# Small operations moved, and the token buffers kept as two pairs, in a two-layer attention kernel

## The chip, the cores and the metric

The kernel runs on one core of one Trainium2 chip. The metric is the device time of one execution in microseconds (us). A program of this kind is timed several times and the median is given; one more execution is recorded by the hardware profiler, and all durations of single instructions below come from that one.

## The reference

The input x has 32 x 128 tokens of 256 channels, all float32. Two layers follow each other.

```python
# layer 0: all 4096 tokens attend to each other, 8 heads of 32 channels
q = layernorm(h) * ln_g + ln_b
q = q @ wq.T + bq + sym_emb[:, None]            # one bias row for each n of 32
Q, K, V = q @ wQ.T + bQ, h @ wK.T + bK, h @ wV.T + bV
scores = Q K^T / sqrt(32);  scores[t_key > t_query] = -inf
h = h + alpha * ((softmax(scores) @ V) @ out_w.T + out_b)

# layer 1: attention in a band of 24 tokens, then a mixture of 8 experts
t = h.reshape(4096, 256)
z = layernorm(t)
logits = relu((z @ K) @ z.T + bias) - 10000 * (1 - band)
t = t + softmax(logits * temperature) @ z
x = layernorm(t);  w = softmax(x @ Wr + br)     # a share of each expert
y_e = relu(bn2(relu(bn1(x @ W1_e + b1_e)) @ W2_e + b2_e)) @ Wo_e + bo_e
t = t + sum_e w_e * y_e
```

## The kernel before

The function fast_kernel does the work; a general one stands by for inputs with large values. The order of instructions is written out by hand: each engine executes its own instructions in the order in which the program issues them, and SyncE (SP) issues nearly all DMAs, in one queue.

**Layer 0.** The 4096 queries, in the order of t, are cut into 8 blocks (b) of 512. A block has two units (b, g), g being one of two groups of four heads, and a unit has steps (b, g, k), k running over the tiles of 128 keys that the mask leaves. For n running over all steps, the loop

- computes scores of step n on TensorE: head 0 into the bank sa, heads 1 to 3 into three banks sb (`scores`, L1330; sb has two buffers);
- adds the products of the weights of step n - 2 with the values into av (`product`, L1420);
- takes the exponentials on ScalarE, in two instructions with `between` in the middle (`exps`, L1343 and L1345), into one of five buffers pt, and clears masked places on GpSimd (L1357). In each unit one step holds two part tiles that both need such clearing, and others hold one;
- adds the weights of step n - 1 on VectorE to an accumulator acc, in two halves of two heads each (`add`, L1371 to L1406). The first addition of a second unit has four parts (L1383, L1387), as it also takes over a tile from the unit before;
- issues one or more pieces of other work, from the generator `todo`, so many per block (`count`), in equal distances.

After a unit has ended, `close_sums` adds the accumulator's rows on TensorE (L1450), and sends them through SP (r16, L1481); five steps later `invert` takes the reciprocals on VectorE (L1489) and sends them through DRAM to all rows (flat, rec), and six steps later `scale` multiplies the result (L1502).

The work in `todo` is first `prep(b + 1)`, in four pieces: the next block is transposed (L984), and its keys, values and queries are projected (L993, L1039, L1012). In block 2 `output_weights` follows: it loads wo_n, alpha and outb, transposes wo_n, scales it by alpha into woT, and then multiplies bvb, the value bias spread over 128 columns, with woT (L1225) to correct outb (L1228). In block 3 `expert_norms` follows: it first calls `window`, which loads two scalars of layer 1 (temp, abias), builds the band bandb on GpSimd (L1237 to L1248) and clears the edges of big_t, then loads the batch norms' vectors, and transposes them in a second piece.

The first two blocks' deviations are computed ahead of layer 0; those of the other 24 tiles in block 1: after the last statistics, `root_rstd` adds 1e-5 on VectorE (L1542) and takes the root on ScalarE (L1545), with an exchange of the activation table before it and after it (L911). `send_rstd` spreads a block's deviations through DRAM (rstd, rb: L972, L976).

**Token buffers.** The pool tok has four buffers under one tag, xg. They hold, in the order of the loads: blocks 0 and 1 for the projections, blocks 2 to 7 for the statistics (named xs), blocks 2 and 3 again, block 4, then wo_n, then blocks 5, 6 and 7, and at last the tokens of layer 1's first four blocks, in which the results are built (tokens0 to tokens3; `load_tokens`, L896). Each load waits until the buffer's last contents were read. `tokens_at` names the steps at which tokens0 to tokens3 are loaded: three in block 5, one in block 6. `with_bias(n)` adds outb to tile n of them on GpSimd (L904): six in block 5, six in block 6, in the second unit, where

```python
if NBLK - 3 <= b < NBLK - 1 and g and 4 <= k < 4 + FIRST // 2:
    with_bias((b - NBLK + 3) * FIRST // 2 + k - 4)
```

**Layer 1.** A stretch written out by hand leads from layer 0 into it. Then 64 pairs of block and expert follow each other (`work`, `Layer`, `combine`), all on TensorE. `combine` multiplies half a block with Wo into one bank (L2137) and adds it to the tokens on VectorE, weighted by the expert's share (L2145); after the last expert it writes each tile out (L2150). Between these products a planner, `insert`, puts the jobs of the later blocks: projection, normalising (ScalarE, L1797), turning (transposes, L1813), keys, band scores, and the jobs that bound the values of the inputs (squares, columns: L2164, L2171). A job is issued once `later` us of the planner's own clock have passed since all that it needs (3.2, and 4.7 from the second block on).

Of the kernel before, what the change touches and what calls it, by code (L numbers as in the profile page):

```python
# [10 lines left out]
F32 = mybir.dt.float32  # L11
# [812 lines left out]
def fast_kernel(ctx: ExitStack, tc: tile.TileContext, ins: dict, out: bass.AP, narrow):  # L824
# [63 lines left out]
    big_t = big.tile([P, 2, NT + 2 * SIDE], F32, name="big_t")  # L888


    tok = ctx.enter_context(tc.tile_pool(name="tok", bufs=4))
# [34 lines left out]
    with ExitStack() as l0:  # L926
# [9 lines left out]
        def load_x(b, name, amid=()):  # L936
            xg = tok.tile([P, TPB, D], F32, tag="xg", name=f"{name}{b}")
            for tl in range(TT):
                if tl < len(amid):
                    amid[tl]()  # L940
                src = x[0][:, b * TPB * TT : (b + 1) * TPB * TT, :].rearrange(
                    "n (i tl) d -> tl n i d", tl=TT
                )[tl]
                nc.sync.dma_start(out=xg[tl * N : (tl + 1) * N], in_=src)
            return xg
# [255 lines left out]
        def output_weights(banks):  # L1201

            wo_n = tok.tile([P, TPB, D], F32, tag="xg", name="wo_n")[:, :2, :]
# [4 lines left out]
            nc.sync.dma_start(out=outb, in_=row(ins["L0_conv_out_b"]).to_broadcast([P, D]))  # L1208
            yield
# [10 lines left out]
            bvb = px.tile([P, 2, P], F32, tag="bvb", name="bvb", bufs=1)  # L1220
            for c in range(2):
                nc.vector.tensor_copy(bvb[:, c, :], colT[:, c, 6:7].to_broadcast([P, P]))
# [10 lines left out]
        def window():  # L1233

            nc.sync.dma_start(out=temp, in_=row(ins["L1_attn_temperature"]).to_broadcast([P, 1]))
            nc.sync.dma_start(out=abias, in_=row(ins["L1_attn_bias"]).to_broadcast([P, 1]))
# [12 lines left out]
            for z in (0, SIDE + NT):  # L1249
                nc.gpsimd.memset(big_t[:, :, z : z + SIDE], 0.0)  # L1250

        def expert_norms(banks):

            window()
# [11 lines left out]
            nc.vector.tensor_copy(bnT.rearrange("p c k -> p (c k)"), ps[:, : 2 * NB])  # L1266
            yield


        with ExitStack() as at:  # L1270
# [91 lines left out]
            def add(b, g, k):  # L1362
# [15 lines left out]
                if k == 1:  # L1378
                    first, lo = held[b, g, 0], parts[0][2]
                    if more:  # L1380
                        z = more[1][2]
                        for hs in HEADS:
# [3 lines left out]
                            )  # L1386
                            nc.vector.tensor_tensor(  # L1387
# [152 lines left out]
            def root_rstd():  # L1540
                cols = slice(2 * TPB, NTILE)
                nc.vector.tensor_scalar(  # L1542
                    rstd0[:, cols], mean0[:, cols, 1], 1e-5, None, op0=ALU.add
                )
# [30 lines left out]
            u, z = NBLK - 3, NBLK - 2  # L1575
            tokens_at = [(u, 0, 2), (u, 0, 4), (u, 1, 0), (z, 1, 0)]
            todo, done, count = iter(()), 0, 0
            later = {}
            for n in range(len(steps) + LAG + 1 + 16):
                if n < len(steps):  # L1580
                    b, g, k = steps[n]
                    own = sum(len(units[b, i]) for i in range(NGRP))
                    if g == 0 and k == 0:
# [9 lines left out]
                        if b == 2:  # L1593
                            todo, count = itertools.chain(todo, output_weights(banks)), 8
                        if b == 3:
                            todo, count = itertools.chain(todo, expert_norms(banks)), 7
# [26 lines left out]
                if n < len(steps):  # L1623
# [12 lines left out]
                    if (b, g, k) in tokens_at:  # L1636
                        nb = tokens_at.index((b, g, k))
                        load_tokens(
                            nb, tok.tile([P, TPB, D], F32, tag="xg", name=f"tokens{nb}")
# [5 lines left out]
                    for sb_, si in stat_at.get(n, ()):  # L1645
                        stats(sb_, si, xstat[sb_])
                        if (sb_, si) == (NBLK - 1, TPB - 1):
                            due = 1
                    if 1 < b < NBLK - 1 and not g and k == 1:
                        send_rstd(b + 1)  # L1650
                    if NBLK - 3 <= b < NBLK - 1 and g and 4 <= k < 4 + FIRST // 2:
                        with_bias((b - NBLK + 3) * FIRST // 2 + k - 4)
# [476 lines left out]
    def combine(ht, k, r2):  # L2129
# [3 lines left out]
        ps = bank(f"psy{k}_{r2}").rearrange("p (k d) -> p k d", k=2)  # L2133
        for i in range(2):
            r = 2 * r2 + i
            for c in range(2):
                nc.tensor.matmul(  # L2137
                    ps[:, i, :], lhsT=ht[:, c, r * P : (r + 1) * P],
# [3 lines left out]
        for i in range(2):  # L2142
# [3 lines left out]
                out=tokens(n), in0=ps[:, i, :], scalar=w[:, r, e : e + 1],  # L2146
# [235 lines left out]
    jobs, done_at = [], {}  # L2382
# [90 lines left out]
    jobs = [j for j in jobs if j[0] not in done_at]  # L2473

# [30 lines left out]
    def insert(passed):  # L2505
# [4 lines left out]
        while k < len(jobs) and few < 3:  # L2510
# [4 lines left out]
            if all(done_at.get(q, now) + later <= now for q in needs if q in known):  # L2515
# [111 lines left out]
```

## Time and profile before

| | us |
|---|---|
| median of 3 runs | 1494.84 (1494.55 to 1494.99) |
| the profiled execution, device time | 1492.53 |
| its span from the first to the last instruction | 1490.7 |
| TensorE (PE) busy in the span | 1457.9 |
| VectorE (DVE) busy | 1201.1 |
| ScalarE (ACT) busy | 936.5 |
| GpSimd (POOL) busy | 159.5 |
| mean granted clock of TensorE | 0.994 of full speed |

In the profile a row of the timeline has the start, the length, the engine, the line, the operation, what it writes and reads, the shape and the count; in brackets stands how long the engine was idle before it, and who ended that. PEld is TensorE's loading of weights, beside its products. SPq and ACTq are the engines' sequencers, which issue DMAs. In this execution block 2 of layer 0 runs from about 96 to 165 us, block 3 to about 246, block 5 from about 339 to 449, block 6 from there to about 577, and layer 1 begins near 710.

### The profile page before, as it was taken

To read this page: it belongs to the slowest core of one execution; us is meant where nothing else is said; L and a number is where in the kernel's file an instruction comes from. 1 tells how busy PE (TensorE), PEld (TensorE's weight loads), DVE (VectorE), ACT (ScalarE), POOL (GpSimd) and SP (SyncE) were. 2 spreads that over 40 slices of the span, in tenths; PEclk is the share of its full clock that TensorE was granted. 3 is DMA by queue.
4 is the path that set the end of the run, shared out by engine and by line. 5 is a ranking of instruction groups with operands and counts; after the bars stand their busy time and mean duration, and the time that the engine had idled before them with its cause. 6 is when DMAs were issued, how large, how long until landed. Compare 5 with 4: busy or idle time off the path is not lost.

```text
span 1490.7 us, 23636 instructions
## 1 busy us (share of the span) xinstructions
PE 1457.9 (98%) x8873; PEld 842.3 (56%) x8873; DVE 1201.1 (81%) x2189; ACT 936.5 (63%) x1357; POOL 159.5 (11%) x318
## 2 busy tenths in 40 slices
PE   9999999999999999999899999999999999999998
PEld 5333232232322232222557888888888888888887
DVE  4777788989999999999746787777777777777775
ACT  4776777879889879989454444445445544544443
POOL 2110112100200200000063012020011000000000
PEclk9999999999999999999999999999999999999999
DMA  6220101021000000000332333333433334334442
GB/s 136 51 45 19 30 10 30 9 41 39 1 15 23 1 9 1 8 9 1 119 119 94 121 121 110 120 115 122 134 112 124 106 121 138 112 121 125 130 148 66
DMA packets 96378, 110.15 MB, mean 74 GB/s; under 512 B 17950, under 2 KB 85233, under 8 KB 96257
## 3 DMA queue, kind: packets, MB, share of 16 engines
q1 hardware_dynamic: 93280, 106.87, 24.2%
q8 instruction: 72, 1.18, 0.4%
q0 software_dynamic: 1888, 0.91, 0.2%
q10 hardware_dynamic: 1088, 0.79, 0.2%
q14 instruction: 50, 0.40, 0.1%
HBM read 98.87 MB, written 8.53 MB: 72 GB/s over the span
## 4 chain that ended last, share of the span: by engine, by line
PE 83%; DVE 9%; ACT 4%; issue 2%; DMA 1%; POOL 1%; SPq 0%; ACTq 0%; DVEq 0%; POOLq 0%
PE psh L2076 22%; PE sa L1330 15%; PE av L1420 15%; PE psy L2137 13%; DVE acc L1406 2%; PE psv L1039 2%; PE psq L1012 2%; PE psk L1825 2%; PE psk L993 2%; PE sums L1450 1%; ACT h L2059 1%; PE sb L1330 1%; PE psh L2081 1%; PE pso L1515 1%; PE pss L1837 1%
## 5 line engine op out<-in xcount | busy, mean ns | idle before, releaser
L1406 DVE TENSOR_TENSOR acc<-acc,pt 128x1024 f32<-128x1024 f32 (+2 forms) x470 | 518.1, 1168 | 31.5 <-POOL pt L1357 16.2
L1345 ACT ACTIVATE pt<-sb 128x1536 f32<-128x1536 f32 (+1 forms) x265 | 382.6, 1444 | 1.7 <-PE sb L1330 1.7
L1330 PE MATMUL sa<-q,kT 32*128 32x512 f32 (+3 forms) x576 | 298.8, 605 | 4.5 <-ACT pt L1343 3.6
L1330 PE MATMUL sb<-q,kT 32*128 32x512 f32 (+3 forms) x1728 | 302.0, 604 | 0.0
L2059 ACT ACTIVATE h<-h,bshift,bscale 128x256 f32<-128x256 f32 x244 | 159.2, 699 | 219.1 <-DVE h L2118 219.0
L1420 PE MATMUL av<-pt,v 128*32 128x512 f32 (+3 forms) x2304 | 284.0, 573 | 3.3 <-POOL pt L1357 2.6
L2137 PE MATMUL psy<-wo,h 128*128 128x256 f32 x1024 | 243.6, 381 | 0.0
L2137 PEld LDWEIGHTS psy<-wo,h 128*128 128x128 f32 x1024 | 191.6, 190 | 31.9 <-issue 5.9
L1330 PEld LDWEIGHTS sa<-q,kT 32*128 32x128 f32 x576 | 86.7, 184 | 211.9 <-ACT pt L1343 176.7
L1343 ACT ACTIVATE pt<-sa 128x512 f32<-128x512 f32 (+1 forms) x265 | 158.2, 597 | 73.2 <-PE sb L1330 44.4
L1420 PEld LDWEIGHTS av<-pt,v 128*32 128x32 f32 x2304 | 48.0, 108 | 202.9 <-issue 178.0
L2145 DVE SCALAR_TENSOR_TENSOR tokens<-psy,w,tokens 128x256 f32<-128x256 f32 x256 | 111.0, 475 | 29.1 <-PE psy L2137 28.7
L2103 DVE TENSOR_TENSOR u<-psh,u 128x256 f32<-128x256 f32 x122 | 51.2, 420 | 100.6 <-ACT u L2102 100.3
L1357 POOL MEMSET pt<- 32x256 f32 (+4 forms) x123 | 52.3, 425 | 603.3 <-ACT pt L1345 526.4
L2059 ACT ACTIVATE h<-psh,bshift,bscale 128x256 f32<-128x256 f32 (+1 forms) x132 | 75.8, 576 | 49.7 <-PE psh L2076 43.3
L1330 PEld LDWEIGHTS sb<-q,kT 32*128 32x128 f32 x1728 | 91.0, 184 | 5.1 <-ACT pt L1345 3.8
L2076 PE MATMUL psh<-tx,s 128*128 128x256 f32 x366 | 89.1, 379 | 0.3 <-DVE tx L2049 0.3
L2102 ACT COPY u<-psh 128x256 f32<-128x256 f32 x122 | 43.9, 361 | 72.0 <-PE psh L2076 71.7
L2076 PE MATMUL psh<-th,s 128*128 128x256 f32 x366 | 89.0, 379 | 0.0
L2118 DVE TENSOR_TENSOR h<-psh,u 128x512 f32<-128x512 f32 x122 | 83.1, 681 | 3.2 <-PE psh L2076 3.0
L2076 PEld LDWEIGHTS psh<-tx,s 128*128 128x128 f32 x366 | 69.4, 190 | 10.2 <-DVE tx L2049 0.7
L2076 PEld LDWEIGHTS psh<-th,s 128*128 128x128 f32 x366 | 69.5, 190 | 9.5
(343 smaller groups left out, 1779.1 us busy)
## 6 DMA issues: line engine op xcount, KB each, us to landing
w<-in_L_ffn_W_dram SPq DMA_DIRECT2D x128, 256.0 KB
s<-kept SPq DMA_DIRECT2D x56, 512.0 KB
wo<-in_L_ffn_Wo_dram SPq DMA_DIRECT2D x64, 256.0 KB
xg<-in_x_dram SPq DMA_DIRECT2D x32, 128.0 KB
tokens<-in_x_dram SPq DMA_DIRECT2D x8, 512.0 KB
kept<-s SPq DMA_DIRECT2D x8, 512.0 KB
out_dram<-tokens SPq DMA_DIRECT2D x32, 128.0 KB
rec<-flat SPq DMA_DIRECT2D x60, 64.0 KB
```

Source lines behind the costliest of these rows:

```text
L1330: nc.tensor.matmul((sb[:, h - 1, :] if h else sa)[:, at : at + w], lhsT=kT[rows, gg, j * P : (j + 1) * P], rhs=q[rows, gg, lo : lo + w], s ...
L1343: nc.scalar.activation(pt[:, 0, used], sa[:, used], AF.Exp, scale=SCALE)
L1345: nc.scalar.activation(pt[:, 1:, used], sb[:, :, used], AF.Exp, scale=SCALE)
L1357: nc.gpsimd.memset(rows, 0.0)
L1406: nc.vector.tensor_tensor(acc[:, hs, cols], acc[:, hs, cols], pt[:, hs, at : at + w], op=ALU.add,)
L1420: nc.tensor.matmul(av[h * HD : (h + 1) * HD, lo : lo + w], lhsT=v[:, j, (g * HG + h) * HD : (g * HG + h + 1) * HD], rhs=pt[:, h, at : at + w],
L2059: nc.scalar.activation(dst, src, AF.Relu, bias=bshift[:, m, k : k + 1], scale=bscale[:, m, k : k + 1])
L2076: nc.tensor.matmul(ps, lhsT=w, rhs=x, start=start, stop=True, skip_group_check=True)
L2103: nc.vector.tensor_tensor(u, a[:, 1], u, op=ALU.add)
L2118: nc.vector.tensor_tensor(flat.rearrange("p (k c) -> p k c", k=2), self.q, self.u.unsqueeze(1).to_broadcast([P, 2, HB]), op=ALU.add,)
L2137: nc.tensor.matmul(ps[:, i, :], lhsT=ht[:, c, r * P : (r + 1) * P], rhs=wo[k][:, c, :], start=(c == 0), stop=(c == 1),)
L2145: nc.vector.scalar_tensor_tensor(out=tokens(n), in0=ps[:, i, :], scalar=w[:, r, e : e + 1], in1=tokens(n), op0=ALU.mult, op1=ALU.add,)
```

## The change

- The pool tok has two tags of two buffers each. The loads go to xa or xb: the statistics' blocks 2, 3, 6 and 7, block 4, wo_n, tokens0 and tokens1 to xb, all others to xa.
- tokens0 and tokens1 are loaded in block 3, and with_bias takes their eight tiles in block 3's second unit (k from 3 to 10). The four tiles of tokens2 follow in block 5's second unit (k from 6 to 9), and none in block 6.
- The first piece of output_weights (its loads, and now the copies to bvb) runs at the start of block 2, and the first piece of expert_norms (its loads, now with temp and abias) at the start of block 3, ahead of that block's own load. window is called after the batch norms' transposes. The edges of big_t are cleared at the program's start.
- The addition of 1e-5 for the 24 tiles is issued directly after their last statistics.
- The four parts of a second unit's first addition stand in another order.
- The last of the 64 pairs uses a bank for each tile in combine.
- The planner waits 4.7 us behind a normalised tile, and 6.0 behind a square.

```diff
+    for z in (0, SIDE + NT):
+        nc.gpsimd.memset(big_t[:, :, z : z + SIDE], 0.0)
-    tok = ctx.enter_context(tc.tile_pool(name="tok", bufs=4))
+    tok = ctx.enter_context(tc.tile_pool(name="tok", bufs=2))
...
         def load_x(b, name, amid=()):
-            xg = tok.tile([P, TPB, D], F32, tag="xg", name=f"{name}{b}")
+            late = b in ((2, 3, 6, 7) if name == "xs" else (4,))
+            xg = tok.tile([P, TPB, D], F32, tag="xb" if late else "xa", name=f"{name}{b}")
...
         def output_weights(banks):
-            wo_n = tok.tile([P, TPB, D], F32, tag="xg", name="wo_n")[:, :2, :]
+            wo_n = tok.tile([P, TPB, D], F32, tag="xb", name="wo_n")[:, :2, :]
...
             nc.sync.dma_start(out=outb, in_=row(ins["L0_conv_out_b"]).to_broadcast([P, D]))
+            bvb = px.tile([P, 2, P], F32, tag="bvb", name="bvb", bufs=1)
+            for c in range(2):
+                nc.vector.tensor_copy(bvb[:, c, :], colT[:, c, 6:7].to_broadcast([P, P]))
             yield
...
             yield
-            bvb = px.tile([P, 2, P], F32, tag="bvb", name="bvb", bufs=1)
-            for c in range(2):
-                nc.vector.tensor_copy(bvb[:, c, :], colT[:, c, 6:7].to_broadcast([P, P]))
             ps = banks("ps_ob", 1)[0][:, :D]
...
         def window():
-            nc.sync.dma_start(out=temp, in_=row(ins["L1_attn_temperature"]).to_broadcast([P, 1]))
-            nc.sync.dma_start(out=abias, in_=row(ins["L1_attn_bias"]).to_broadcast([P, 1]))
...
-            for z in (0, SIDE + NT):
-                nc.gpsimd.memset(big_t[:, :, z : z + SIDE], 0.0)
         def expert_norms(banks):
-            window()
+            nc.sync.dma_start(out=temp, in_=row(ins["L1_attn_temperature"]).to_broadcast([P, 1]))
+            nc.sync.dma_start(out=abias, in_=row(ins["L1_attn_bias"]).to_broadcast([P, 1]))
...
             nc.vector.tensor_copy(bnT.rearrange("p c k -> p (c k)"), ps[:, : 2 * NB])
+            window()
             yield
...
                                 live[b, g][:, hs, :z], first[:, hs, :z], pt[:, hs, :z],
                                 op=ALU.add,
                             )
+                        for hs in HEADS:
                             nc.vector.tensor_tensor(
                                 live[b, g][:, hs, z:], live[b, g][:, hs, z:], pt[:, hs, z:],
...
             def root_rstd():
                 cols = slice(2 * TPB, NTILE)
-                nc.vector.tensor_scalar(
-                    rstd0[:, cols], mean0[:, cols, 1], 1e-5, None, op0=ALU.add
-                )
...
-            u, z = NBLK - 3, NBLK - 2
-            tokens_at = [(u, 0, 2), (u, 0, 4), (u, 1, 0), (z, 1, 0)]
+            tokens_at = [(3, 0, 2), (3, 0, 9), (NBLK - 3, 1, 0), (NBLK - 2, 1, 0)]
...
                         if b == 2:
-                            todo, count = itertools.chain(todo, output_weights(banks)), 8
+                            more = output_weights(banks)
+                            next(more)
+                            todo, count = itertools.chain(todo, more), 7
                         if b == 3:
-                            todo, count = itertools.chain(todo, expert_norms(banks)), 7
+                            more = expert_norms(banks)
+                            next(more)
+                            todo, count = itertools.chain(todo, more), 6
...
                         nb = tokens_at.index((b, g, k))
+                        tag = "xb" if nb < 2 else "xa"
                         load_tokens(
-                            nb, tok.tile([P, TPB, D], F32, tag="xg", name=f"tokens{nb}")
+                            nb, tok.tile([P, TPB, D], F32, tag=tag, name=f"tokens{nb}")
                         )
...
                         if (sb_, si) == (NBLK - 1, TPB - 1):
+                            cols = slice(2 * TPB, NTILE)
+                            nc.vector.tensor_scalar(
+                                rstd0[:, cols], mean0[:, cols, 1], 1e-5, None, op0=ALU.add
+                            )
                             due = 1
...
-                    if NBLK - 3 <= b < NBLK - 1 and g and 4 <= k < 4 + FIRST // 2:
-                        with_bias((b - NBLK + 3) * FIRST // 2 + k - 4)
+                    if b == NBLK - 5 and g and 3 <= k < 3 + 2 * TPB:
+                        with_bias(k - 3)
+                    if b == NBLK - 3 and g and 6 <= k < 6 + FIRST - 2 * TPB:
+                        with_bias(2 * TPB + k - 6)
...
-        ps = bank(f"psy{k}_{r2}").rearrange("p (k d) -> p k d", k=2)
+        if k < len(work) - 1:
+            ps = bank(f"psy{k}_{r2}").rearrange("p (k d) -> p k d", k=2)
+            pss = [ps[:, i, :] for i in range(2)]
+        else:
+            pss = [bank(f"psy{k}_{r2}_{i}")[:, :D] for i in range(2)]
...
+    for name in bound_of:
+        slow["square", name] = 6.0
+    for n in range(NTILE):
+        slow["normalise", n] = 4.7
...
-            if all(done_at.get(q, now) + later <= now for q in needs if q in known):
+            if all(done_at.get(q, now) + max(later, slow.get(q, 0)) <= now for q in needs if q in known):
```

More of the change, by code (lines that the diff above doesn't have):

```diff
@@ L2137, in combine @@
                 nc.tensor.matmul(
-                    ps[:, i, :], lhsT=ht[:, c, r * P : (r + 1) * P],
+                    pss[i], lhsT=ht[:, c, r * P : (r + 1) * P],
                     rhs=wo[k][:, c, :],
@@ L2145, in combine @@
             nc.vector.scalar_tensor_tensor(
-                out=tokens(n), in0=ps[:, i, :], scalar=w[:, r, e : e + 1],
+                out=tokens(n), in0=pss[i], scalar=w[:, r, e : e + 1],
                 in1=tokens(n), op0=ALU.mult, op1=ALU.add,
@@ L2377, in fast_kernel @@
         with_bias(n)
-    jobs, done_at = [], {}
+    jobs, done_at, slow = [], {}, {}
     def job(name, cost, f, *needs):
```

## The prediction

> **What bounds the kernel now.** I read the page's first two parts, then the waits, then the timeline around each wait of TensorE, and last the table of stretches with the granted clock. The page says that TensorE is the bound everywhere:
>
> ```profile
> PE 1457.9 (98%) x8873; PEld 842.3 (56%) x8873; DVE 1201.1 (81%) x2189; ACT 936.5 (63%) x1357; POOL 159.5 (11%) x318
> PEclk9999999999999999999999999999999999999999
> ```
>
> So a moved small operation can only pay where TensorE stands idle (1490.7 - 1457.9 = 32.8 us, 6.9 of it after the last product), or where it is busy at a low clock, which the tenths hide. The timeline shows the idle places by the bracket behind a TensorE row. The five large ones of layer 0:
>
> ```profile
> 72.61 0.69 PE L1330 MATMUL sa<-q,kT 32*128 32x512 f32 x1 [2.04 <-ACT pt L1343]
> ...
> 145.57 0.63 PE L1213 MATMUL ps_wo<-ident,wo_n 128*128 128x128 f32 x4 [1.97 <-DMA wo_n<-in_L_conv_out_w_dram]
> ...
> 157.00 2.04 PE L1225 MATMUL ps_ob<-woT,bvb 128*128 128x256 f32 x4 [3.01 <-DVE bvb L1222]
> ...
> 232.25 1.51 PE L1420 MATMUL av<-pt,v 128*32 128x384 f32 x8 [2.61 <-POOL pt L1357]
> ...
> 521.31 0.69 PE L1330 MATMUL sa<-q,kT 32*128 32x512 f32 x1 [0.84 <-ACT pt L1343]
> ```
>
> What stands behind the first, the fourth and the fifth is one engine further back: ScalarE waits for an addition that VectorE has behind its sums, GpSimd is held by the band, and ScalarE waits for a buffer that VectorE has not yet read.
>
> ```profile
> 69.18 0.22 ACT L1545 ACTIVATE rstd<-rstd 128x24 f32<-128x24 f32 x1 [2.06 <-DVE rstd L1542]
> ...
> 222.66 7.25 POOL L1246 TENSOR_SCALAR bandb<-bandb,abias 128x160 f32<-128x160 f32 x1 [12.82 <-DMA abias<-in_L_attn_bias_dram]
> ...
> 520.66 0.60 ACT L1343 ACTIVATE pt<-sa 128x512 f32<-128x512 f32 x1 [1.60 <-DVE acc L1383]
> ```
>
> The stretches just after three of these waits carry a second loss. Their columns are length, busy time by engine, then the granted clock (0.50 here, 1.00 around them):
>
> ```profile
> 146.47:149.88 3.41, 3.41 (x28) 1.10 (x20) 2.76 (x3) 2.30 (x4) 0.00 (x0) 0.50 0.00 0
> 156.71:160.12 3.41, 3.12 (x12) 1.69 (x12) 1.31 (x6) 0.00 (x0) 0.00 (x0) 0.50 0.00 0
> 231.80:238.63 6.83, 6.38 (x38) 1.76 (x40) 6.26 (x8) 1.94 (x2) 0.40 (x1) 0.50 0.46 116
> ```
>
> TensorE is busy in them, and does half the work: they cost another 1.71, 1.56 and 3.19 us (half of the busy time).
>
> [...] idle times of 1.94 to 2.98 us were enough, while the 2.04 us at 70.6 drew nothing. [...] the band's addition (L1246) took 7.25 us beside a run of VectorE sums, and VectorE's 0.68 us halves (L1387) took 1.21 us beside the bias additions of L904 at 513 to 520. [...] the trace has 1.28 for both loads around the root (L1545, L911). The change keeps their number.
>
> **The change part by part**, each against the profiled execution.
>
> 1. *The addition of 1e-5 before the root* (L1542) goes directly behind the last statistics, which ended at 64.14. ScalarE's first table load ends at 65.84 + 1.28 = 67.12, so its 2.06 us wait goes; the second load and the key copies come as much earlier, and TensorE's 2.04 us with them. Next late is nothing above 0.1: the products before end at 70.57, and the exponential would then end at about 70.5. Gain 2.0 (1.2 to 2.1).
>
> 2. *wo_n loaded at block 2's start* instead of inside it: 1.94 + 1.71 = 3.65. Its three issues (0.58, 0.47, 0.43) now stand on SP ahead of the load of xg4, the exchange of deviations and the row sums; those rows are read by VectorE at 120.2, and were issued by 109.8, so 1.5 us are covered.
>
> 3. *bvb copied at block 2's start*: 2.98 + 1.56 = 4.54. The copies (0.36) only change their place on VectorE. But something is late next. The projection's bank is released by L1228, which in the new order stands behind the three sums of a masked step. From that step's scores: exponentials end at 3.3, the masks' memset (1.63) at 4.95, three sums (some 2.7) at 7.6, L1228 (0.48) at 8.1; TensorE, with 2.07 per step and 0.85 for the projection, wants the bank at 7.1. I charge 1.0 (0 to 2). Net of parts 2 and 3: 7.2.
>
> 4. *The band built late, its two scalars loaded early.* The masks' memset of the step at 226 no longer queues behind L1246: 2.61 + 3.19 = 5.80. The band (0.24 + 0.54 + 0.66 + up to 7.25 + 0.44) runs after that memset, with 14 us until the next.
>
> 5. *Tokens 0 and 1 and eight bias additions into block 3.* Four stand on GpSimd from 208, four around the band. They took 0.74 us each, the worst 3.24. They slow VectorE's sums as at 513; there, six of them cost TensorE 0.84 through ScalarE's wait. Block 3 has more cover (VectorE is busy for 76.1 of the 90.1 us from 158.9 to 249; in blocks 5 and 6 for about 97%), and the new order of the four split sums frees the awaited buffer one sum (0.69) sooner. Charge 0.5 (0 to 2). Block 6 loses its six: gain 0.8 (0 to 1.0). Block 5 keeps four of six: nothing.
>
> 6. *SP in block 3.* Twelve small loads (219.29 to 223.81, 4.5 us) come ahead of xg5, and tokens0 ahead of the row sums; it waits for the transposes of xg4 (over at 177.4), no longer than SP waits for the deviations anyway (until 172.9, then 177.4). The row sums were issued by 178.15 and read at 185.09; with 1.4 us to land (from flat to rec: 185.37 to 186.79) there are 5.5 us, and 4.5 plus up to 1.0 for the tokens use them up. What is over goes into VectorE's lag, which five exponential buffers cover. Nothing, bound 0 to 3.
>
> 7. *The pool as two pairs* keeps four buffers. Apart from tokens0 each load waits for a reader of a block or more before. The edges' memset (0.18) moves to GpSimd's start. Nothing.
>
> 8. *Planner.* Two idle places of TensorE before turns of normalised tiles (0.50 and 0.81, at 785 and 786) should go, as those turns move behind other products; the 0.56 before L2171 at 770 stays, since that job keeps its place. Reordering can open a new one: 1.0 (-1 to 1.3).
>
> 9. *The last expert in separate banks.* VectorE's last pair (0.88, from 1483.92) starts when the last four products are done; now its first half runs beside the last two, and the end comes one half (0.44) sooner. Gain 0.4.
>
> Sum: 2.0 + 7.2 + 5.8 - 0.5 + 0.8 + 1.0 + 0.4 = 16.7 us. The profiled execution took 1492.53 (1490.7 and 1.8 around it), so 1475.8 for it; the median shown is 2.3 higher, 1494.84, and becomes **1478.1**. With all charges at their good ends about 1475, at their bad ends 1482.
>
> **The rivals.**
>
> *The waits come back as smaller ones.* In a full step ScalarE has 0.60 + 1.45 = 2.05 of TensorE's 2.07 us, and VectorE two sums of 1.16. The stalls of blocks 2 and 3 also let these two catch up. For it: ScalarE idled up to 1.7 us just there. Against it: both have 15% and more free over blocks 2 and 3. It would give back half: about 1486. Chance 0.2.
>
> *The half rate isn't tied to these stalls*, but moves to other small ones; the 2.04 us at 70.6 without a penalty speaks for it. Then 6.5 us stay: 1484.6. Chance 0.1.
>
> *GpSimd locked out, slower.* In block 3 the queue between the masks at 229 and those at 243 holds the band's addition and four bias additions. With the worst durations seen it takes 4 x 3.24 + 7.25 + 1.9 = 22.1 us, 8 too long, and the gain shrinks by 8 and a half-rate window. It turns into a loss when the five take over some 6 us each: 33 us, 19 late, 3.4 at half rate, about 1500. For it: VectorE runs sums without a break there. Against it: 0.74 was the median in busier blocks. Chance 0.04.
>
> *The change doesn't reach the path* (the loads still late, stalls as long): within 0.2%. Chance 0.02.
>
> **The numbers.** The main case has 0.64, its own range 1475 to 1482. The range of 1473.5 to 1486 takes in the first two rivals, and a little for another chip. Under 0.2% (3 us) no measurement of this kernel tells a change from none. Faster 0.94, same 0.02, slower 0.04.
>
> **What would show it.** Right: no 0.50 stretch between 10 and 700 us; the idle rows above gone before L1213, L1225 and the av rows of block 3; TensorE's busy time down by some 6 us although its work is the same; ScalarE's root without a wait. Wrong: a new row on SP or VectorE with over 3 us of waiting in block 3, a GpSimd row of L906 near 7 us, or idle TensorE before scores in block 2.

## The result and the profile after

Before: 1494.91 us, median of 4 runs (1494.55 to 1495.11). Changed: **1481.20 us**, median of 4 (1479.99 to 1482.25). The ratio is 0.9908 [0.9891, 0.9925], 13.7 us less. The profiled execution took 1482.25, the longest of the four. A second set of runs of the same kernel (after_again) gave 1480.09 (1479.08 to 1481.51), ratio 0.9906 [0.9889, 0.9923], and a profiled span of 1477.6.

The page's first part, of the changed kernel:

```profile
PE 1456.1 (98%) x8873; PEld 842.4 (57%) x8873; DVE 1197.2 (81%) x2189; ACT 937.0 (63%) x1357; POOL 156.7 (11%) x318
```

TensorE's timeline, changed kernel, in the order of the rows shown of before (length of the row behind its start, idle time ahead of it in the bracket):

```profile
71.38 0.69 PE L1331 MATMUL sa<-q,kT 32*128 32x512 f32 x1
...
140.08 0.66 PE L1219 MATMUL ps_wo<-ident,wo_n 128*128 128x128 f32 x4
...
146.97 1.13 PE L1228 MATMUL ps_ob<-woT,bvb 128*128 128x256 f32 x4
...
221.85 1.07 PE L1422 MATMUL av<-pt,v 128*32 128x384 f32 x16
...
228.36 2.04 PE L1331 MATMUL sb<-q,kT 32*128 32x512 f32 x6 [1.25 <-DVE bnT L1266]
...
511.93 0.69 PE L1331 MATMUL sa<-q,kT 32*128 32x512 f32 x1
```

All five idle places are gone: the rows have no bracket. One new row has one: scores of block 3 wait 1.25 us for a bank of PSUM, which psbn held until VectorE had copied it to bnT.

ScalarE's timeline at the root, changed kernel: the root follows its table load without a wait.

```profile
66.66 1.28 ACT L1544 ACT_TABLE_LOAD   x1
67.95 0.22 ACT L1544 ACTIVATE rstd<-rstd 128x24 f32<-128x24 f32 x1
```

The table of stretches, changed kernel (length, busy time and count of PE, PEld, DVE, ACT and POOL, granted clock): the new wait drew the one stretch at half rate between 10 and 700 us. The second profile has the same wait (1.24) and no such stretch at all.

```profile
225.03:228.44 3.41, 2.17 (x16) 0.50 (x13) 3.31 (x5) 2.05 (x2) 3.24 (x3) 1.00 0.69 196
228.44:231.86 3.42, 3.42 (x14) 0.59 (x14) 3.42 (x4) 1.41 (x1) 3.35 (x4) 0.50 0.17 18
```

**Where the time went.** TensorE's first product into `sums` after each unit (L1450 before, L1452 after) is a mark that both kernels have. The differences between marks, taken from the two timelines, give the gain by stage:

| stage | before, us | predicted | changed | changed, second profile |
|---|---|---|---|---|
| start to block 0's end | 48.52 | 0 | +0.82 | -0.10 |
| block 1, first unit | 34.06 | -2.0 | -2.06 | -2.06 |
| block 2 | 69.43 | -7.2 | -7.56 | -7.56 |
| block 3 | 81.03 | -5.3 | +0.29 | -1.39 |
| block 6, second unit | 65.30 | -0.8 | -0.90 | -0.90 |
| layer 1, first to 129th product of combine | 108.97 | -1.0 | -1.00 | -1.00 |
| from the last product of combine to the span's end | 7.25 | -0.4 | +0.08 | -0.06 |
| all others | | 0 | +0.05 | -0.07 |
| span | 1490.7 | -16.7 | -10.3 | -13.1 |

Apart from the start, every line but block 3's came out within 0.5 us. The start differs by up to 1 us between executions of any of the kernels (the first scores began between 18.3 and 19.7). Block 3 is what the experiments are about.

### The profile page after: what moved, and what is told of

It is laid out like the page before. It is cut to its first block, busy times and chain, and to the rows that moved or that the text cites. A ratio compares the mean times of both kernels' runs of the same rounds, so it can differ in the third digit from the quotient of the medians.

```text
span 1480.5 us, 23640 instructions
## 1 busy us (share of the span) xinstructions
PE 1456.1 (98%) x8873; PEld 842.4 (57%) x8873; DVE 1197.2 (81%) x2189; ACT 937.0 (63%) x1357; POOL 156.7 (11%) x318
## 3 DMA queue, kind: packets, MB, share of 16 engines
q8 instruction: 72, 1.18, 0.4%
## 4 chain that ended last, share of the span: by engine, by line
PE 86%; DVE 8%; ACT 3%; issue 2%; DMA 1%; ACTq 0%; DVEq 0%
PE psh L2085 22%; PE sa L1331 16%; PE av L1422 16%; PE psy L2151 13%; PE psv L1042 2%; PE psk L996 2%; PE psq L1015 2%; PE psk L1834 2%; PE sums L1452 2%; PE sb L1331 2%; DVE acc L1408 2%; ACT h L2068 1%; PE psh L2090 1%; PE pso L1517 1%; PE pss L1846 1%
```

## The experiments

Twelve kernels were run, each beside the kernel before on its chip. Two groups come at the question from both sides: the first four from the changed kernel, the next six from the kernel before; the last two carry the finding on.

| run | median, us | ratio to before, 95% |
|---|---|---|
| after_again | 1480.09 | 0.9906 [0.9889, 0.9923] |
| a1_bnT_act | 1481.48 | 0.9908 [0.9891, 0.9924] |
| a2_pieces7 | 1480.39 | 0.9906 [0.9890, 0.9923] |
| a3_both | 1479.61 | 0.9903 [0.9887, 0.9920] |
| b1_tokens | 1495.22 | 1.0007 [0.9998, 1.0016] |
| b2_weights | 1487.06 | 0.9952 [0.9935, 0.9968] |
| b2a_load | 1489.39 | 0.9970 [0.9959, 0.9982] |
| b3_band | 1491.96 | 0.9986 [0.9977, 0.9994] |
| b4_root | 1490.65 | 0.9981 [0.9972, 0.9990] |
| b5_planner | 1492.83 | 0.9999 [0.9990, 1.0007] |
| c1_band_block2 | 1480.31 | 0.9908 [0.9893, 0.9923] |
| c2_spread | 1479.44 | 0.9898 [0.9883, 0.9913] |

### From the changed kernel: is it the bank, or the place of a piece of work?

**after_again** is the changed kernel without an edit.

> The changed kernel once more, as the reference for the next three on one chip. All theories: 1480 to 1482.5 us; TensorE idle about 1.25 us before a score of block 3 (released by the copy bnT, L1266), and one stretch of 3.41 us at a granted clock of 0.50 behind it, unless the stretch falls elsewhere in this execution: the spread of 2.3 us among four executions is about one such stretch of 1.7 us lost.

**a1_bnT_act** takes the copy that releases the bank off VectorE:

```diff
-            nc.vector.tensor_copy(bnT.rearrange("p c k -> p (c k)"), ps[:, : 2 * NB])
+            nc.scalar.copy(bnT.rearrange("p c k -> p (c k)"), ps[:, : 2 * NB])
```

> The changed kernel with the copy of the transposed batch norms (bnT) on ScalarE instead of VectorE. Theory 1 (the bank of psbn is held by a copy that stands behind VectorE's sums of the masked step): TensorE's 1.25 us and the stretch at 0.50 in block 3 go, 3 us less than the changed kernel, about 1478. Rival (ScalarE and VectorE are both used up after the masked step, whoever copies): the wait comes back under a ScalarE row, within 1 us of the changed kernel.

**a2_pieces7** spreads block 3's other work over seven pieces, as before the change, so that the projection of the next queries (psq, 3.7 us of TensorE) stands in the first unit again:

```diff
             nc.vector.tensor_copy(bnT.rearrange("p c k -> p (c k)"), ps[:, : 2 * NB])
+            yield
             window()
...
-                            todo, count = itertools.chain(todo, more), 6
+                            todo, count = itertools.chain(todo, more), 7
```

> The changed kernel with block 3's pieces of other work in the places of before (count 7), the band as a seventh piece of its own at its old step, bnT on VectorE. Theory 1: psbn now stands ahead of the masked step, its copy is some two sums late and no more, so the wait is under 0.5 us without a stretch at 0.50, and the queries' projection (psq) again covers ScalarE's work at the unit's start, where the changed kernel loses 0.8 to 1.1 us: together 3 to 4 us less than the changed kernel. Rival (bias additions of GpSimd slow VectorE's sums there): they stay where they are, so the loss at the unit's start stays too, at most 3 us less.

**a3_both** has both edits.

> Both edits: pieces in the places of before and bnT on ScalarE. Theory 1: about 4 us less than the changed kernel, 1477, and no stretch at 0.50 between 10 and 700 us. Rival: no better than the better one of the two single edits, or within 1 us of the changed kernel.

Measured: no median differs from the changed kernel's by more than the runs scatter. In the traces the wait for the bank is gone in all three, and others stand in its place. In a1 the sums at 240.36 wait 2.10 us; the profile names ScalarE's exponentials as the releaser there, as that run's rival had it, but VectorE has no break either from 212 us to the unit's end. TensorE's timeline in a3_both (a2 has the same two waits, 1.35 and 1.41):

```profile
234.89 1.06 PE L1423 MATMUL av<-pt,v 128*32 128x512 f32 x8 [1.35 <-POOL pt L1359]
...
239.60 2.10 PE L1453 MATMUL sums<-acc,ones 128*32 128x512 f32 x8 [1.40 <-DVE acc L1409]
```

The second row's releaser is VectorE's last sum of the unit. VectorE is late there, and taking one wait of TensorE away only makes it wait at the next place. Block 3 gains 1.80, 2.12 and 2.12 us against the kernel before in a1, a2 and a3, where the changed kernel's second profile has 1.39: the bank's 1.25 us were worth 0.4, the place of psq 0.7. In a1, 1.2 us are given back in block 4, behind a half-rate stretch at 240.2, and 1.7 in layer 1, behind another at 762.

### From the kernel before: one part at a time

**b1_tokens**: the two pairs of buffers, the loads and the bias additions, and nothing else.

```diff
-    tok = ctx.enter_context(tc.tile_pool(name="tok", bufs=4))
+    tok = ctx.enter_context(tc.tile_pool(name="tok", bufs=2))
...
-            tokens_at = [(u, 0, 2), (u, 0, 4), (u, 1, 0), (z, 1, 0)]
+            tokens_at = [(3, 0, 2), (3, 0, 9), (NBLK - 3, 1, 0), (NBLK - 2, 1, 0)]
...
-                    if NBLK - 3 <= b < NBLK - 1 and g and 4 <= k < 4 + FIRST // 2:
-                        with_bias((b - NBLK + 3) * FIRST // 2 + k - 4)
+                    if b == NBLK - 5 and g and 3 <= k < 3 + 2 * TPB:
+                        with_bias(k - 3)
+                    if b == NBLK - 3 and g and 6 <= k < 6 + FIRST - 2 * TPB:
+                        with_bias(2 * TPB + k - 6)
```

> The kernel before with the token part alone: two pairs of buffers, tokens0 and tokens1 loaded in block 3, eight bias additions there, four in block 5, none in block 6. The working of the prediction: block 6's idle 0.84 us before L1330 goes (0.8 less), block 3 pays 0.5 (0 to 2) through slower sums; net -0.3, between -0.9 and +1.5. In block 3 the band still stands in GpSimd's queue and waits for its scalar, so the masks may come later than before: up to +3. Rival (the token move is what pays): 3 us less or more.

Block 6 is 0.90 shorter, as in the changed kernel; block 3 is 2.18 longer. GpSimd's and TensorE's timelines in b1_tokens show one reason: two additions now stand between the band and the masks, and TensorE's wait for these grew from 2.61 to 3.98.

```profile
223.46 7.22 POOL L1247 TENSOR_SCALAR bandb<-bandb,abias 128x160 f32<-128x160 f32 x1 [10.56 <-DMA abias<-in_L_attn_bias_dram]
...
231.26 1.40 POOL L904 TENSOR_TENSOR tokens<-tokens,outb 128x256 f32<-128x256 f32 x2
232.72 1.63 POOL L1358 MEMSET pt<- 32x256 f32 x3
```

```profile
234.40 1.94 PE L1421 MATMUL av<-pt,v 128*32 128x384 f32 x16 [3.98 <-POOL pt L1358]
```

The other reason is on VectorE: its five sums behind the masks took 5.02 us in the kernel before, and beside the four additions that follow them

```profile
234.38 6.83 DVE L1407 TENSOR_TENSOR acc<-acc,pt 128x768 f32<-128x768 f32 x5 [4.09 <-POOL pt L1358]
```

So the token move alone loses 1.3 us in the two blocks. With the band's new place it gains little: block 3 is 2.10 shorter with the band alone (b3_band, below) and 1.39 with the additions too, which takes 0.7 of block 6's 0.9.

**b2_weights**: wo_n loaded and bvb copied at block 2's start. **b2a_load**: the load alone, bvb where it was. The lines below are the whole edit of b2a_load; b2_weights also moves the copies, as in the diff of the change.

```diff
                         if b == 2:
-                            todo, count = itertools.chain(todo, output_weights(banks)), 8
+                            more = output_weights(banks)
+                            next(more)
+                            todo, count = itertools.chain(todo, more), 7
```

> The kernel before with wo_n loaded and bvb copied at the start of block 2, nothing else. The working of the prediction: 7.2 us less (6.2 to 8.2), without the stretches at a granted clock of 0.50 at 146 and 157 us. Rival (the half rate is not tied to these waits): it turns up elsewhere in blocks 1 to 3, and 4 us less are measured.

> The kernel before with the loads of output_weights at the start of block 2, and the copies to bvb where they were. Working: the first of the two stalls and its half rate go, 1.94 + 1.71 = 3.65 less; the second stall of 2.98 us stays, with 1.5 of half rate. Rival: as VectorE then comes to its copies with a longer queue, the second stall grows and less than 2 are left.

b2_weights shortens block 2 by 7.48, b2a_load by 1.87. With the load alone, the wait for bvb grew from 3.01 to

```profile
152.06 2.04 PE L1225 MATMUL ps_ob<-woT,bvb 128*128 128x256 f32 x4 [3.56 <-DVE bvb L1222]
```

The two moves pay together: a gain of 3.65 and one of 4.54 were worked out, and the first alone brings half of its own. VectorE comes to its copies later, as the rival of that run had it.

b2a_load is also the run that settles block 3. It has the old 2.60 us wait for the masks there, and no half-rate stretch behind it; the kernel before has the same wait and 6.83 us at half rate. Block 3's second unit is shorter by only **0.99 us**, where half of TensorE's busy time, 3.19, was counted. In b2_weights, b4_root and b5_planner the same wait drew one cell of 3.41 us at half rate instead of two, and the unit is shorter by the same 0.99: one cell costs nothing there, and only the second one costs. The cover is VectorE's. Its timeline around the masks and at the unit's end, first of the kernel before:

```profile
232.23 5.02 DVE L1406 TENSOR_TENSOR acc<-acc,pt 128x768 f32<-128x768 f32 x5 [2.72 <-POOL pt L1357]
237.17 0.32 DVE L1266 COPY bnT<-psbn 128x160 f32<-128x160 f32 x1
237.40 9.16 DVE L1406 TENSOR_TENSOR acc<-acc,pt 128x1024 f32<-128x1024 f32 x8
246.48 1.25 DVE L1502 TENSOR_TENSOR big_t<-big_t,rec 128x512 f32<-128x512 f32 x1
247.63 2.35 DVE L1406 TENSOR_TENSOR acc<-acc,pt 128x1024 f32<-128x1024 f32 x2
251.36 2.36 DVE L1398 TENSOR_TENSOR acc<-pt,pt 128x1024 f32<-128x1024 f32 x2 [1.38 <-ACT pt L1345]
```

Then of b2a_load:

```profile
230.57 5.02 DVE L1406 TENSOR_TENSOR acc<-acc,pt 128x768 f32<-128x768 f32 x5 [2.71 <-POOL pt L1357]
...
248.72 2.36 DVE L1398 TENSOR_TENSOR acc<-pt,pt 128x1024 f32<-128x1024 f32 x2 [0.39 <-ACT pt L1345]
```

VectorE stands still for 2.7 us at the masks, too, and then runs without a break to the unit's end. While it works its backlog off, TensorE at half rate loses little. VectorE's wait at the end falls from 1.38 to 0.39: these are the 0.99 us.

**b3_band**: the band's part alone.

```diff
         def expert_norms(banks):
-            window()
+            nc.sync.dma_start(out=temp, in_=row(ins["L1_attn_temperature"]).to_broadcast([P, 1]))
+            nc.sync.dma_start(out=abias, in_=row(ins["L1_attn_bias"]).to_broadcast([P, 1]))
...
             nc.vector.tensor_copy(bnT.rearrange("p c k -> p (c k)"), ps[:, : 2 * NB])
+            window()
```

> The kernel before with the band's part alone: the scalars and batch norms loaded at block 3's start, the band built behind the batch norms' transposes. Prediction: 5.8 us less. Theory 1: the bank of psbn is late then too, behind it another stretch at 0.50, so only 1 to 3 us less. A difference of under 3 shows that the masks' wait had covered the wait for the copy to bnT.

Block 3 is 2.10 shorter, and has no half-rate stretch; the masks' wait is gone, and a wait of 0.49 for the bank of psbn stands there instead. By the reckoning of b2a_load, 2.61 + 0.99 = 3.6 could be had. The band's new place beside VectorE's sums does not take the rest: the thirteen sums behind the reciprocal took 14.32 us, against 14.18 in the kernel before.

```profile
233.69 5.16 DVE L1406 TENSOR_TENSOR acc<-acc,pt 128x768 f32<-128x768 f32 x5
...
239.00 9.16 DVE L1406 TENSOR_TENSOR acc<-acc,pt 128x1024 f32<-128x1024 f32 x8
```

The place of psq and the bank of psbn may take most of it; in the changed kernel they were worth 0.7 and 0.4 (a2, a1). The other 0.4 stays open. The 1.63 us that block 1 lost in this execution belong to a half-rate stretch behind the old stall of the root (below).

**b4_root**: the addition of 1e-5 moved, and nothing else. **b5_planner**: the planner's new waiting times alone.

```diff
             def root_rstd():
                 cols = slice(2 * TPB, NTILE)
-                nc.vector.tensor_scalar(
-                    rstd0[:, cols], mean0[:, cols, 1], 1e-5, None, op0=ALU.add
-                )
...
                         if (sb_, si) == (NBLK - 1, TPB - 1):
+                            cols = slice(2 * TPB, NTILE)
+                            nc.vector.tensor_scalar(
+                                rstd0[:, cols], mean0[:, cols, 1], 1e-5, None, op0=ALU.add
+                            )
```

> The kernel before with only the addition of 1e-5 before the root moved behind the last statistics. Theory: the 2.06 us wait of ScalarE at 69.2 and the 2.04 us of TensorE at 70.6 go; block 1 is 2.0 shorter, ratio 0.9986, the rest as before. Rival, the stall is only put off to the next late thing in block 1: 0 to -1. A half-rate stretch of 3.41 us drawn or not drawn in some executions can add or hide 1.7.

> The kernel before with only the planner's new waiting times (6.0 us after a tile's squares, 4.7 after a normalised tile). Theory: the two idle places of TensorE at 785 and 786 (0.50 and 0.81) go and one of about 1.4 that was there before stays or moves, the first stage of layer 1 is 1.0 shorter, ratio 0.9993. Rival, the new order opens a wait as long as those it closes: within 0.3 of the kernel before, ratio 1.000. With the kernel before at 1494.5 the two are 1 us apart, near what five rounds can tell; the stage's length in the trace decides rather than the median.

b4_root shortens block 1's first unit by 2.05, ratio 0.9981: 2.7 us by the medians. For b5_planner the medians don't tell (0.9999). The traces do in part: both runs drew one half-rate stretch, of 3.41 us, among the first 128 products of combine, and that stage became 1.61 longer in b4_root (old planner) and 0.69 longer in b5_planner: the planner is worth 0.92 by this pair. Over all traces it is a range: with such a stretch the stage is 1.38 and 1.61 longer under the old planner and 0.67 to 0.69 under the new one; without one the old planner's four traces lie between 0.40 shorter and 0.08 longer, and those of the new one are all 1.00 shorter. That makes 0.6 to 1.1. TensorE's two idle places at 785 and 786 are gone in b5_planner, and one of the same kind as in the changed kernel is new:

```profile
849.07 1.13 PE L1890 MATMUL psa<-xl,ptl 128*128 128x256 f32 x4 [1.44 <-ACT ptl L1881]
```

The idle times above 0.2 us of that stage add up to 2.88 before and 2.72 in the changed kernel, so most of the 1.0 is not in them, but in less busy time of TensorE for the same products (105.92 and 105.21). Why the other order of products takes less was not tried.

### What is next late in block 3?

**c1_band_block2** takes a3_both and moves the band to block 2, **c2_spread** also moves the last four of block 3's bias additions behind that block's last step, into block 4's part of the program (GpSimd executes them from 232.6 us on, around the border of the two blocks):

```diff
+                    if (b, g, k) == (2, 0, 5):
+                        window()
...
-                    if b == NBLK - 5 and g and 3 <= k < 3 + 2 * TPB:
+                    if b == NBLK - 5 and g and 3 <= k < 3 + TPB:
                         with_bias(k - 3)
+                    if b == NBLK - 4 and not g and 3 <= k < 3 + TPB:
+                        with_bias(TPB + k - 3)
```

> The changed kernel with the copy of bnT on ScalarE and the unused seventh piece of block 3 kept (both as in a3_both), and the band taken out of block 3: its two scalars are loaded at block 2's start and GpSimd builds it behind the masks of block 2's fifth step (about 112 us), where it has 14 us free. In a3_both two waits are left in block 3: 1.35 us before the product at 233.5 (masks that stand behind two bias additions, the band and two more additions on GpSimd) and 1.37 us before the sums at 238.2 (VectorE's sums late). Theory, GpSimd's queue is what took the place of the old stall: the 1.35 goes altogether, and of the 1.37 at least half, since 6.5 us of GpSimd work beside VectorE's sums are gone; block 3 shortens by 2.0 (1.4 to 2.7) against a3_both, about 1477.6, ratio to the kernel before 0.989. Rival, VectorE's own sums are the bound there: the masks' wait goes but the wait before the sums grows by as much, and the time stays at 1479.6 (0.990). Block 2 may pay 0 to 1 for the band.

> c1_band_block2 with the last four of block 3's eight bias additions moved into the first half of block 4. Theory: with no GpSimd work but masks and four early additions in block 3, both waits there are gone, 2.7 us less than a3_both in block 3; block 4 pays 0 to 0.6 (six additions in block 6 were worth 0.9). 1476.9 to 1478, ratio 0.988 to 0.989. Rival, the additions cost nothing in block 3 once the band is away: equal to c1_band_block2 within 0.3. Rival, VectorE's own sums are the bound: 1479.6.

In c1_band_block2 the masks' wait of 1.35 goes, and the one before the sums grows from 1.40 to 2.31, as the rival had it:

```profile
239.69 2.84 PE L1452 MATMUL sums<-acc,ones 128*32 128x512 f32 x8 [2.31 <-DVE acc L1408]
```

Block 3 gains 2.65 against the kernel before; a half-rate stretch at 240.9 then takes 1.87 back in block 4. In c2_spread the masks' wait is gone, too, the one before the sums is smaller and in two parts, and block 3 gains 3.99:

```profile
237.88 1.05 PE L1452 MATMUL sums<-acc,ones 128*32 128x512 f32 x4 [1.00 <-DVE acc L1408]
...
239.46 1.05 PE L1452 MATMUL sums<-acc,ones 128*32 128x512 f32 x4 [0.53 <-DVE acc L1408]
```

The four additions then slow VectorE around the border, and block 4 loses 0.76 (0.22 in a3_both), so 3.2 are left. VectorE's timeline holds the price. The thirteen sums behind the reciprocal of this unit, in the second profile of the changed kernel, beside additions and band:

```profile
221.22 5.92 DVE L1408 TENSOR_TENSOR acc<-acc,pt 128x768 f32<-128x768 f32 x5
227.05 0.32 DVE L1266 COPY bnT<-psbn 128x160 f32<-128x160 f32 x1
227.29 10.25 DVE L1408 TENSOR_TENSOR acc<-acc,pt 128x1024 f32<-128x1024 f32 x8
```

and in c2_spread, without either:

```profile
220.90 14.11 DVE L1408 TENSOR_TENSOR acc<-acc,pt 128x768 f32<-128x768 f32 x13 [0.91 <-POOL pt L1358]
```

They take 16.17 and 14.11 us; in the kernel before it was 5.02 + 9.16 = 14.18. **GpSimd's work costs VectorE 2.0 us there, and VectorE has no break.** It is the additions that cost this, not the band. With the band alone it was 14.32 (b3_band), and with four additions and no band, in c1_band_block2,

```profile
221.37 15.93 DVE L1408 TENSOR_TENSOR acc<-acc,pt 128x768 f32<-128x768 f32 x13 [0.90 <-POOL pt L1358]
```

The single sums say the same: in the second profile two full sums beside the last two additions took 1.75 and 1.76 us, the full ones beside the band's addition 1.22 and 1.23.

The account of block 3 then comes near: 3.6 to be had, less 2.0, leaves 1.6, and the second profile gained 1.39. Without the 2.0, and with the copy to bnT (0.32) on ScalarE, it would be 3.9, and c2_spread gained 3.99. It does not close everywhere: the same reckoning gives 3.5 for b3_band, which gained 2.10, and 2.2 for c1_band_block2, which gained 2.65. By the medians c2_spread, with 0.9898 [0.9883, 0.9913], can't be told from the changed kernel.

## Why the prediction was right, and where it was off

The predicted median was 1478.1, the measured one 1481.2, within the range given; the main case came true, with a gain of 13.7 in place of 16.7. The range of the main case, 1475 to 1482, is not the sum of the ends that the parts were given: these add up to gains of 18.8 and 7.6, or about 1476 and 1487. For the profiled execution the sum said 1475.8; it took 1482.25, and the one of the second profile 1479.49. Errors hardly made up for one another: outside block 3 (and the start) the parts gave 11.6 in the second profile, where 11.4 were predicted, and nearly all that is missing is missing in block 3.

- **Step 1, the root**: 2.0 predicted, 2.06 in the changed kernel and 2.05 alone (b4_root). The wait did not come back later.
- **Steps 2 and 3**: 7.2 net, 7.56 measured. The term for the bank of the projection was 1.0; scores at 150 us had to wait about 0.6 for it (sb starts at 150.76, behind the end of VectorE's L1231 at 150.70; its sa starts at 150.12, in the steps before the two are 0.01 to 0.02 apart). b2a_load shows that the two steps may not be priced one by one.
- **Step 4, the band, is the most mis-sized one**: 5.8 predicted, 2.10 alone (b3_band). Of its two terms, the 3.19 for the half rate were worth 0.99 (b2a_load and three more runs), so 3.6 were to be had. And the prediction took "VectorE is busy for 76.1 of the 90.1 us" for cover, an average: from 212.84 to 249.98 of the kernel before VectorE has one break only, the 2.72 us at the masks, which is the wait that was to go. With that closed and the additions in its place VectorE sets the end of the unit, as a3_both and c1_band_block2 show. The wait for the bank of psbn (1.25), released by VectorE behind its sums, is one way in which this shows on TensorE. The same mechanism had been named for L1228 in block 2, and was not looked for at L1266.
- **Step 5, the bias additions**, is too small: a charge of 0.5 in block 3. The last four alone cost VectorE 1.8 us (15.93 against 14.11). On the length of block 3 the additions' part is 0.7 by one comparison (2.10 for the band alone, 1.39 with the additions), and 1.3 for the last four by another (c2_spread against c1_band_block2). One reading was wrong: 0.74 us is the median of all 32 additions of the kernel; the twelve of blocks 5 and 6 took 1.18 in the median. They were charged by the six at 513, with a discount for the cover of block 3, which this unit doesn't have once the masks' wait is gone. Block 6: 0.8 predicted, 0.90 measured, and nothing in the five runs that leave the additions there.
- **Steps 6 and 7**, SP's queue and the pairs of buffers: nothing predicted. The row sums do come late in block 3's first unit, and VectorE waits 2.13 us for them (L1491, at 178.5), where it had no such wait before. TensorE has no wait in that unit, whose length is unchanged in a2 and a3, so it was covered, as predicted; that the five exponential buffers did it was not tested.
- **Step 8, the planner**: 1.0 predicted, 1.00 measured (0.6 to 1.1 over all traces), but not by the working given: the 1.31 of two idle places went, and 1.44 of a new one came. The size is luck.
- **Step 9, the last bank**: 0.4 predicted. VectorE's last operation does end earlier, 0.52 us behind TensorE's last product instead of 0.92, but the four issues of the output on SP took 3.53 us instead of 2.53, and the end did not move. It was not run alone.

Of the rivals, **the waits that come back as smaller ones** came true in block 3 alone. **The half rate that isn't tied to these stalls** came true in part. In 14 traces every such stretch follows idle time of TensorE; but with the stalls gone, stretches turned up behind other idle places in four of the seven traces of kernels with the whole change (at 228, 240 and 241, and 759 to 762 us), the first profile among them, and the sign "no 0.50 stretch between 10 and 700 us" held only in the second profile of the changed kernel. **GpSimd locked out** did not happen: block 3's additions took 0.7 to 2.1 us each in the changed kernel, and the band's addition 2.66, against the 3.24 and 7.25 assumed for it. What did happen is the reverse, GpSimd's additions slowing VectorE. TensorE's busy time was to fall by some 6 us; it fell by 1.8, and by 4.1 in the second profile (1453.8). Part of the six was the 3.19 of block 3, which had not been a loss of that size.

## What to carry to other kernels

A wait of the bounding engine is worth its length only as far as the next engine is ahead (the band's part was priced at 5.80 us and gave 2.10): look at that engine's rows from the wait to the end of the stage, not at its share of the block, and ask whether its only break is the wait that you remove. Where a moved operation releases a bank or a buffer, find every such releaser and what stands in front of it on its engine. Two operations that hold one queue in turn (here the band and the additions, the load and the copies) are to be priced together, since each alone may gain little or nothing (the load alone gave 1.87 us, load and copies 7.48). Work that moves to an idle engine can still slow the engine beside it (thirteen sums of VectorE took 16.17 us beside GpSimd's additions and band, 14.11 without them): compare the neighbour's single rows with and without it.

## What the runs showed of the hardware

**Half-rate stretches sit on a grid.** In each trace the stretches between changes of the granted clock are multiples of 3.413 us, counted from its first record and leaving out the last one, which the trace's end cuts off (139.946 us at full rate before the first one in the kernel before are 41 of them, 221.866 in the changed kernel 65). Inside the half-rate stretches of the kernel before, a second group of four products of 128x512 into av started 0.84 us behind the first (two cases), elsewhere between 30 and 700 us 0.43 in the median. TensorE's timeline, cut by this grid, gives for each cell how long TensorE stood idle in it. The kernel before, around the root's wait of 2.04 us, cut in two by the border at 71.38:

```profile
67.96:71.38 3.42, 2.61 (x26) 0.88 (x24) 3.42 (x5) 2.17 (x4) 0.00 (x0) 1.00 0.35 77
71.38:74.79 3.41, 2.18 (x17) 0.58 (x18) 0.24 (x2) 3.41 (x6) 0.80 (x2) 1.00 0.07 1
74.79:78.20 3.41, 3.41 (x16) 2.84 (x16) 1.92 (x5) 0.94 (x1) 1.25 (x4) 1.00 0.06 5
```

The same wait in b3_band, in one cell, with the next one at half rate:

```profile
71.60:75.01 3.41, 1.42 (x12) 0.47 (x16) 1.00 (x2) 3.40 (x7) 0.07 (x1) 1.00 0.13 20
75.01:78.42 3.41, 3.41 (x13) 1.82 (x6) 1.17 (x3) 1.70 (x2) 1.97 (x5) 0.50 0.07 5
```

Over the 14 traces, between 30 and 700 us, each of the 15 cells at full rate with 1.95 us or more of idle TensorE was followed by a cell at half rate; of the 19 with 1.0 to 1.8 us, one was (the changed kernel's at 225.03, above). So the 2.04 us at the root drew a stretch in one of six traces, and the 2.60 at the masks in four of five. In layer 1 idle time alone does not decide: 0.90 us in one cell, near 760, drew one in all five traces that had it, while 1.31 near 785 (six traces) and 1.37 to 1.44 near 835 (eight traces) drew none. The exceptions fall into line when the time is added in which TensorE is busy with little: 0.89 us near 760, of products of one column (L2171), and 0.90 at 225.03, of head 0's scores alone, while the other heads' had no bank. Counted so, in all cells at full rate between 30 and 1460 us, 16 of 16 with 1.95 us or more drew a cell at half rate, five of the seven with 1.79, and none with less. This count was made after the fact, and no run tested it. In these traces a stall near 2 us cost its length, and in some executions up to half a cell more (1.63 us in block 1 of b3_band; half of 3.41 is 1.7). One or two such cells are as much as the runs of one kernel scatter (2.3 us for the changed kernel, 4.4 for the kernel before, from the shortest to the longest). The runs' own clocks point the same way: of the 23 runs of the kernel before beside c2_spread, the six with a mean clock of 0.993 have spans of 1492.5 to 1493.8 us, and the four with 0.996 have 1489.4 to 1491.4. That these cells make up the whole scatter was not shown.

**A wait on one side, a slower pace on both.** The band's addition of 128x160 took 7.17 to 7.25 us in the six traces that have it at its old place beside a run of VectorE's sums, and ended each time 0.39 us behind the reciprocal that closes the run; the sums beside it kept their 1.22 us. It took 2.58 to 2.66 in the changed kernel and a1 to a3, 1.27 in b3_band, and in block 2, where VectorE has a break (c1_band_block2):

```profile
113.51 1.00 POOL L1249 TENSOR_SCALAR bandb<-bandb,abias 128x160 f32<-128x160 f32 x1
```

The bias additions of 128x256 took 0.72 us alone. The first of a group took longer in the same way in places (3.23 us at 395.0 in the kernel before, 4.03 at 232.6 in c2_spread); behind it additions and sums ended by turns, with 1.17 to 1.72 for an addition and 1.75 instead of 1.22 for a full sum. Why the band's addition ended behind six sums in a row in one place and behind fewer in another, no run here tested.
